# A conditioned block on one core: where the last pair's quarter r3 is summed and gated

## The chip, the cores and the metric

The kernel runs on one core of a Trainium2 chip. The metric is device time in microseconds for one launch; the figure given is the median of several runs. The core's engines are TensorE (PE; its weight loads are shown as PEld), VectorE (DVE), ScalarE (ACT), GpSimd (POOL) and SyncE (SP). SP and ACT issue the transfers.

## The reference

The inputs are `x` of 2 x 2048 x 512 and a condition of 2 x 512, all float32. Cut to what matters:

```python
emb = jnp.dot(jax.nn.silu(t), ada_w) + ada_b
shift_msa, scale_msa, gate_msa, shift_mlp, scale_mlp, gate_mlp = jnp.split(emb, 6, axis=-1)
norm = _ln(x) * (1.0 + scale_msa[:, None]) + shift_msa[:, None]
h = jax.nn.gelu(jnp.dot(norm, ssm_w1) + ssm_b1, approximate=False)
x = x + gate_msa[:, None] * (jnp.dot(h, ssm_w2) + ssm_b2)
norm2 = _ln(x) * (1.0 + scale_mlp[:, None]) + shift_mlp[:, None]
hf = jax.nn.gelu(jnp.dot(norm2, ff_w1) + ff_b1, approximate=True)     # 512 -> 1024
x = x + gate_mlp[:, None] * (jnp.dot(hf, ff_w2) + ff_b2)              # 1024 -> 512
```

The change touches the last line.

## The kernel before, in words

**Tiling.** The 4096 rows of `x` are eight blocks of 512 rows. The first part of the kernel carries each block through the first two products (`ssm1`, `ssm2`). Then the feed-forward part (`ff`) takes the blocks in four pairs, s = 0 to 3: for each pair `up(s)` makes the 1024 hidden columns, and `down(s)` multiplies them by `fw2`. The last pair is s = 3, in the code `last`.

**Fewer products.** Every large product is a 2 x 2 product of quarters done in seven multiplications instead of eight, by Strassen's scheme in Winograd's form, and each of the seven is again done in seven: these inner multiplications are called leaves. In `down` the outer seven run in the order of `DOWN`, P1, P2, P3, P6, P5, P7, P4; the leaves of each run in the order P1, P5, P6, P2, P7, P3, P4. The leaves of two neighbouring outer products alternate on TensorE. A leaf of `down` is two matmuls into a 128 x 256 piece of a PSUM bank. The inner scheme adds some leaves onto others within the bank; six of the seven are read out afterwards. `QUAD` says to which quarter (e, h) of the result each leaf is added. A quarter is complete with the leaf P2, P7, P3 or P4.

**The four sums.** The outer results are collected in `summed`, in SBUF, with the feature on the partitions: r0 is the first half of the output features (d = 0) for the pair's first block, r1 the second half (d = 1) of the first block, r2 d = 1 of the second block, and r3 d = 0 of the second block. Under P1, r1 is set. Under P2, r0 = r1 + P2 is done. Under P3, r3 = P3 is set. Under P6, r1 = r1 + P6. Under P5, r2 = r1 + P5, and when a quarter is complete, r3 = r3 + r2. P7 and P4 end r2 and r1.

**Outputs.** `quarter_out(s, d, blk, r)` sends a finished sum: two passes on ACT apply the gate (scale) and the gated bias (the two values of `columns`), two block transposes on DVE write a band in the tile `far`, four stores write the band to DRAM (`back`), one load brings it back turned (tile `rows`), two additions add the rest of `x` (in `far` or `near`), and the result is stored. In the last pair r0 and r3 go this way, with stores spread over SP and ACT (`queue`). r1 and r2 of the last pair are gated ahead of P7 and P4 by one ACT pass over both, and the leaves of P7 and P4 are then added by `scaled_add`, a multiply-add on DVE that reads the leaf from PSUM. TensorE turns their pieces as they are complete (`turned_by_pe`); DVE adds them to the rest of `x` in the tile `hidden`, and each piece is stored.

**Order.** No order is written by hand. Every instruction is added to `Plan` with the engines that could take it ("vg" is DVE or POOL), a cost in ns, and what it reads and writes. `Plan.order` gives each instruction a latest time, counted back from TensorE's matmuls, whose order is fixed, and from the closing stores, and then simulates the engines: on each engine the instruction with the earliest latest time goes first among those that are ready. A price of `AHEAD` is put on work that DVE could leave to POOL. Additions on DVE and POOL with both inputs in SBUF are kept from running at the same time (`shared`). Each engine then works through its list in that order.

Lines of the profile: L258 is `tt` (additions on DVE or POOL), L276 is `act`, L285 `copy`, L296 `mm`, L306 `turn_by_pe`, L318 `dma`, L1049 `scaled_add`, L1073 the block transposes of `quarter_out`.

Of the kernel before, what the change touches and what calls it, by code (L numbers as in the profile page):

```python
# [11 lines left out]
AF = mybir.ActivationFunctionType  # L12
ALU = mybir.AluOpType
# [187 lines left out]
def kernel(  # L201
# [42 lines left out]
    def cols(ap):  # L244
        n = 1
        for d in ap.shape[1:]:
            n *= d
        return n

    def in_psum(*aps):  # L250
        return any("PSUM" in str(a.space) for a in aps)

    def tt(e, o, a, b, f):
        n, ps = cols(o), in_psum(a, b)
        cost = {"v": n / 0.96 + 70, "g": 2.12 * n + 145}
        plan.add(
            e,
            lambda E: E.tensor_tensor(o, a, b, f),  # L258
            [o],
            [a, b],  # L260
            cost,
            {"v": cost["v"] + 85, "g": cost["g"] + 45},
            "g" if ps else "vg",
        )
# [5 lines left out]
    def act(o, a, func, bias=0.0, scale=1.0):  # L270
        n = cols(o)
        ptrs = [p for p in (bias, scale) if not isinstance(p, float)]
        cost = n / 1.4 + (155, 215, 340)[len(ptrs)]
        plan.add(
            "a",
            lambda E: E.activation(o, a, func, bias=bias, scale=scale),  # L276
            [o],
            [a] + ptrs,
            {"a": cost},
            {"a": cost + 90},  # L280
        )
# [31 lines left out]
    def dma(o, a, q="s", lead=0.0, lat=2000.0, sooner=0.0):  # L313
        size = max(cols(o.unsqueeze(0)), 1) * 4
        outs = [o] if o.tensor.name in scratch else []
        ins = [a] if a.tensor.name in scratch else []
        lead = lead or (0.0 if ins or not outs or size <= plan.LITTLE else 25000.0)
        plan.add(q, lambda E: E.dma_start(out=o, in_=a), outs, ins, {q: plan.ISSUE}, {q: lat}, size=size, lead=lead)  # L318
        plan.ops[-1].sooner = sooner
# [27 lines left out]
    def cut(t, form, **sizes):  # L347
        return t.rearrange(form, **sizes)
# [6 lines left out]
    for n in range(8):  # L355
        t = psum.tile([P, 2 * HT], F32, tag=f"bank{n}", name=f"bank{n}")
# [61 lines left out]
    def thirds(t):  # L418
        return [t[:, n] for n in range(3)]
# [545 lines left out]
    def chain_banks(n):  # L965
        b = {"y": banks[Y_AT[n % 4]], "x": banks[X_AT[n % 2]], "v": banks[V_AT[n % 2]]}
        return b
# [75 lines left out]
    quarters = [0]  # L1043

    def scaled_add(o, t, scale):
        cost = cols(o) / 0.96 + 70
        plan.add(
            "v",
            lambda E: E.scalar_tensor_tensor(o, t, scale, o, ALU.mult, ALU.add),  # L1049
            [o],  # L1050
            [t, o, scale],
            {"v": cost},
            {"v": cost + 85},
        )

    def columns(s, d, e, blk):
        k, b = 2 * d + e, (2 * s + blk) // PER_B
        return gb5[:, k, b : b + 1], mods[5][:, k, b : b + 1]

    def rest_in(s, d, blk, x):  # L1060
        half = slice(d * D // 2, (d + 1) * D // 2)
        dma(x, x1_d[2 * s + blk][:, :, half])
        return x, out_blk[2 * s + blk][:, :, half]

    def quarter_out(s, d, blk, r):
        done = summed[:, r]
        n = quarters[0] % 2
        for e in range(2):
            act(done[:, e], done[:, e], AF.Identity, *columns(s, d, e, blk))
        band = cut(bands[n], "p (a c e r) -> p e c a r", a=M, c=C, e=2)  # L1070
        for e in range(2):
            o, a = band[:, e], cut(done[:, e], "p (c a q) -> p c a q", c=C, a=M)
            plan.add("v", lambda E, o=o, a=a: E.transpose(o, a), [o], [a], {"v": 636}, {"v": 705})  # L1073
        closing = s + 1 == NBLK // 2
        queue = lambda f: "sa"[f % 2] if closing else "s"
        far_t = back_d[s][d][blk]
        for f in range(M):
            dma(far_t[:, f].rearrange("(a q) r -> q a r", a=M), cut(bands[n][f * G : (f + 1) * G], "p (a r) -> p a r", a=M), queue(f))
        flat = done.rearrange("p e t -> p (e t)")
        dma(flat, far_t.rearrange("p f r -> p (f r)"))  # L1080
        x, to = rest_in(s, d, blk, rest[n])
        for h in range(2):
            c = slice(2 * h, 2 * h + 2)
            o = cut(x[:, c], "p c (e f r) -> p (c e) f r", e=2, f=M)
            a = cut(flat, "p (f c e r) -> p c e f r", f=M, c=C, e=2)[:, c].rearrange("p c e f r -> p (c e) f r")
            tt("v" if closing else "vg", o, a, o, ALU.add)
            if closing:
                dma(to[:, c], x[:, c], queue(h))
                plan.closing.append(plan.ops[-1].n)
        if not closing:  # L1090
            dma(to, x)
        quarters[0] += 1

    def down(s):
        q = {f"{o + 1}{blk + 1}": hC[:, blk, :, 2 * o : 2 * o + 2, :] for o in range(2) for blk in range(2)}
        ops = {"P1": q["11"], "P2": q["21"], "P3": q["22"]}
        inner = {}
        last = s + 1 == NBLK // 2

        def sums():  # L1100
            plan.stage = f"ff2 {s}"
            a, b, c = whole_s
            parts("vg", a, q["12"], q["11"], ALU.subtract, 2)
            parts("vg", b, q["22"], a, ALU.subtract, 2)
            parts("vg", q["12"], q["22"], q["12"], ALU.subtract, 2)
            ops.update(P4=c, P5=a, P6=b, P7=q["12"])

        def last_sum():
            plan.stage = f"ff2 {s}"
            parts("vg", ops["P4"], q["21"], ops["P6"], ALU.subtract, 2)  # L1110

        def prepare(n):
            w = ops[DOWN[n]]
            v = {f"{k + 1}{h + 1}": w[:, k, :, h * HT : (h + 1) * HT] for k in range(2) for h in range(2)}
            inner[n] = second(v, thirds(half_s[n % 2]), room=rooms[n % 3] if n < 4 else None)

        def leaf(n, f):
            p = DOWN[n]
            bank = chain_banks(14 * s + 7 + n)
            t = bank[BANK[f]][:, :HT]  # L1120
            for k in range(2):
                mm(t, fw2_leaves[p][f][:, k, :], inner[n][f][:, k, :], f in ("P1", "P5") and k == 0, f in ("P2", "P3", "P4") and k == 1)
            if f == "P1":
                copy(bank["x"][:, :HT], t)
                return
            quad = QUAD[f]
            e, h = int(quad[0]) - 1, int(quad[1]) - 1
            new = f not in ("P7", "P3")
            part = summed[:, :, e, h * HT : (h + 1) * HT]
            r0, r1, r2, r3 = [part[:, r] for r in range(4)]  # L1130

            def add(o, a):
                tt("v", o, t, a, ALU.add)

            if p in ("P1", "P3"):
                o = r1 if p == "P1" else r3
                if new:
                    copy(o, t)
                else:
                    add(o, o)  # L1140
            elif p == "P2":
                add(r0, r1 if new else r0)
                if f == "P4":
                    quarter_out(s, 0, 0, 0)
            elif p == "P6":
                add(r1, r1)
            elif p == "P5":
                add(r2, r1 if new else r2)
                if f in ("P2", "P7", "P3", "P4"):
                    tt("vg", r3, r3, r2, ALU.add)  # L1150
                    if last:
                        act(part[:, 1:3], part[:, 1:3], AF.Identity, *columns(s, 1, e, 0))
                if f == "P4":
                    quarter_out(s, 0, 1, 3)
            elif p == "P7":
                both, wide = part[:, 1:3], t.unsqueeze(1).to_broadcast([P, 2, HT])
                if last:
                    scaled_add(both, wide, columns(s, 1, e, 0)[1])
                else:
                    tt("v", both, wide, both, ALU.add)  # L1160
                if last:
                    turned_by_pe(1, 2, f, quad)
                elif f == "P4":
                    quarter_out(s, 1, 1, 2)
            elif not last:
                add(r1, r1)
                if f == "P4":
                    quarter_out(s, 1, 0, 1)
            else:
                scaled_add(r1, t, columns(s, 1, e, 0)[1])  # L1170
                turned_by_pe(0, 1, f, quad)

        return sums, last_sum, prepare, leaf
# [198 lines left out]
    for i in range(1, NBLK):  # L1372
# [4 lines left out]
        last = i + 2 >= NBLK  # L1377
# [64 lines left out]
```

## Time and profile before

| what | value |
|---|---|
| median of 3 runs | 565.63 us (565.54 to 566.38) |
| the profiled execution | 565.75 us, its span 564.0 us |
| granted TensorE clock, mean | 0.998 |
| PE / DVE / POOL / ACT busy | 98% / 85% / 69% / 50% of the span |
| moved by DMA | 123.68 MB, 219 GB/s in the mean |

The span is the time from the first to the last event of the profiled execution. The busy shares are means over stages with different limits. In rows of the timeline the first number is the start in us from the span's begin, the second the time until the group's end; "x2" merges neighbouring instructions of one kind; the bracket gives the idle time ahead of it and what ended it.

### The profile page before, as it was taken

What the parts mean: (1) busy time and instruction counts of PE and PEld (TensorE: products, weight loads), DVE (VectorE), ACT (ScalarE), POOL (GpSimd) and SP (SyncE); (2) the same over time, 40 slices, a digit from 0 to 9 for tenths busy, and PEclk for the clock granted to TensorE, in tenths of its full rate; (3) what the DMA queues carried; (4) which work ended last, traced back from release to release, by engine and by line L of the source; (5) the groups of instructions that cost most, each with busy time, mean ns of one, the idle gap of its engine ahead of it and who ended that gap; (6) DMA issues with size and microseconds to landing.
All of it is one profiled execution on the core that took longest, in us unless ns stands there. A gap on an engine that the chain in (4) does not pass through costs nothing.

```text
span 564.0 us, 8729 instructions
## 1 busy us (share of the span) xinstructions
PE 552.8 (98%) x2809; PEld 481.2 (85%) x2809; DVE 481.4 (85%) x842; ACT 281.7 (50%) x521; POOL 388.5 (69%) x475
## 2 busy tenths in 40 slices
PE   8999999999999999999999999999999999999994
PEld 4888889888898988888878888888888888888883
DVE  5696978888778588899999997799988999988896
ACT  3474867674877855556206347315338314335230
POOL 2887747979935399984746777676768677767650
PEclk9999999999999999999999999999999999999999
DMA  8953799988399969994202899602998503984317
GB/s 314 399 223 84 239 347 308 331 257 269 103 289 327 302 272 265 329 284 159 74 2 53 295 328 336 190 4 69 317 318 308 183 9 103 319 267 144 95 36 224
DMA packets 66033, 123.68 MB, mean 219 GB/s; under 512 B 5652, under 2 KB 33220, under 8 KB 64452
## 3 DMA queue, kind: packets, MB, share of 16 engines
q1 hardware_dynamic: 63696, 121.53, 65.5%
q10 hardware_dynamic: 2292, 1.60, 1.0%
q8 instruction: 22, 0.36, 0.2%
q14 instruction: 23, 0.19, 0.1%
HBM read 77.89 MB, written 44.18 MB: 216 GB/s over the span
## 4 chain that ended last, share of the span: by engine, by line
PE 87%; DVE 7%; DMA 3%; ACT 1%; issue 1%; POOL 1%; DVEq 0%; SPq 0%; ACTq 0%
PE bank L296 87%; DVE rows L258 2%; DMA fw<-in_L_cond_ada_w_dram 1%; DVE near L258 1%; DVE rows L1049 1%; DVE fw L258 1%; DMA rows<-back 1%; DVE far L258 1%; DVE far L1073 1%; ACT rows L276 1%; DVE hidden L258 0%; DMA fw<-in_L_cond_ada_b_dram 0%; PE bank L306 0%; POOL hidden L258 0%; POOL near L258 0%
## 5 line engine op out<-in xcount | busy, mean ns | idle before, releaser
L296 PE MATMUL bank<-turned,ring 128*128 128x256 f32 x896 | 210.2, 380 | 0.2 <-DVE turned L660 0.2
L296 PEld LDWEIGHTS bank<-turned,ring 128*128 128x128 f32 x896 | 167.9, 190 | 23.2 <-DVE turned L660 0.4
L258 DVE TENSOR_TENSOR hidden<-bank,hidden 128x512 f32<-128x512 f32 (+2 forms) x178 | 126.2, 738 | 23.8 <-PE bank L296 20.3
L296 PE MATMUL bank<-near,hidden 128*128 128x256 f32 (+1 forms) x470 | 95.1, 350 | 0.0
L296 PEld LDWEIGHTS bank<-near,hidden 128*128 128x128 f32 x470 | 82.2, 190 | 9.4 <-POOL near L258 0.3
L258 POOL TENSOR_TENSOR turned<-turned 128x512 f32<-128x512 f32 (+1 forms) x65 | 73.6, 1145 | 22.3 <-DVE turned L258 10.2
L296 PE MATMUL bank<-far,fw 128*128 128x256 f32 (+1 forms) x354 | 86.0, 374 | 0.2
L296 PE MATMUL bank<-ring 128*128 128x256 f32 x336 | 82.7, 380 | 0.1
L258 DVE TENSOR_TENSOR rows<-bank,rows 128x256 f32<-128x256 f32 (+1 forms) x142 | 66.0, 478 | 15.5 <-PE bank L296 12.6
L296 PEld LDWEIGHTS bank<-far,fw 128*128 128x128 f32 x354 | 66.5, 190 | 9.6 <-POOL fw L258 0.5
L285 ACT COPY bank<-bank 128x512 f32<-128x512 f32 (+2 forms) x84 | 37.7, 449 | 73.6 <-PE bank L296 67.1
L296 PEld LDWEIGHTS bank<-ring 128*128 128x128 f32 x336 | 63.5, 190 | 9.9 <-ACT bank L285 0.5
L258 POOL TENSOR_TENSOR hidden<-hidden 128x128 f32<-128x128 f32 (+2 forms) x46 | 46.9, 1029 | 28.4 <-DVE hidden L258 13.3
L276 ACT ACTIVATE hidden<-hidden,cols 128x512 f32<-128x512 f32 (+1 forms) x66 | 44.4, 709 | 42.2 <-DVE hidden L258 42.1
L296 PE MATMUL bank<-near,fw 128*128 128x256 f32 (+1 forms) x246 | 60.6, 376 | 0.0
L296 PE MATMUL bank<-hidden,fw 128*128 128x256 f32 (+1 forms) x216 | 53.3, 376 | 0.2
L296 PEld LDWEIGHTS bank<-near,fw 128*128 128x128 f32 x246 | 46.3, 190 | 6.1
L276 ACT ACTIVATE turned<-turned,mod,mod 128x512 f32<-128x512 f32 x56 | 42.4, 807 | 8.7 <-DMA turned<-turned 8.3
L296 PEld LDWEIGHTS bank<-hidden,fw 128*128 128x128 f32 x216 | 40.2, 190 | 6.3 <-issue 0.9
L258 POOL TENSOR_TENSOR fw<-fw 128x256 f32<-128x256 f32 (+1 forms) x38 | 35.6, 945 | 11.5 <-DMA fw_parts<-fw 4.0
L258 POOL TENSOR_TENSOR ring<-turned,ring 128x256 f32<-128x256 f32 x41 | 29.8, 739 | 16.8 <-PE bank L296 14.6
L276 ACT ACTIVATE rows<-rows,gb,mod 128x512 f32<-128x512 f32 x32 | 25.7, 812 | 27.0 <-DVE rows L258 18.8
(123 smaller groups left out, 734.3 us busy)
## 6 DMA issues: line engine op xcount, KB each, us to landing
ring<-fw_parts SPq DMA_DIRECT2D x28, 512.0 KB, 4.1
turned<-far SPq DMA_DIRECT2D x52, 256.0 KB, 4.0
ring<-fw_parts SPq DMA_DIRECT2D x28, 384.0 KB, 5.4
turned<-turned SPq DMA_DIRECT2D x32, 256.0 KB, 5.1
rows<-back SPq DMA_DIRECT2D x14, 512.0 KB, 5.9
back<-far SPq DMA_DIRECT2D x52, 128.0 KB, 3.0
fw_parts<-fw SPq DMA_DIRECT2D x21, 256.0 KB, 4.9
fw<-in_L_cond_ada_w_dram SPq DMA_DIRECT2D x5, 1024.0 KB
```

The costliest lines, as they stand in the source:

```text
L258: lambda E: E.tensor_tensor(o, a, b, f),
L276: lambda E: E.activation(o, a, func, bias=bias, scale=scale),
L285: plan.add("a", lambda E: E.copy(o, a), [o], [a], {"a": cost}, {"a": cost + 60})
L296: lambda E: E.matmul(o, lhsT, rhs, start=start, stop=stop, skip_group_check=True, **kw),
L1049: lambda E: E.scalar_tensor_tensor(o, t, scale, o, ALU.mult, ALU.add),
L1073: plan.add("v", lambda E, o=o, a=a: E.transpose(o, a), [o], [a], {"v": 636}, {"v": 705})
```

## The change

In the last pair, when a quarter of r1 = P1 + P6 is complete (under P6), r3 += r1 is done at once, on DVE or POOL, and an ACT pass applies gate and bias to that quarter of r3. Under P5 each leaf is then read twice from PSUM: by a multiply-add onto r3 (`scaled_add` with the gate of d = 0 and the second block), and by the addition into r2 as before. The addition r3 += r2 and the two ACT passes in `quarter_out` for r3 fall away in the last pair. The other pairs keep their instructions. Two costs of the planner are changed: a tanh Gelu pass by +30 ns, a `scaled_add` by +50 ns (in all pairs). The order of all engines is planned anew from this.

```diff
@@ act
-        cost = n / 1.4 + (155, 215, 340)[len(ptrs)]
+        cost = n / 1.4 + (155, 215, 340)[len(ptrs)] + (30 if func == AF.Gelu_apprx_tanh else 0)
@@ scaled_add
-        cost = cols(o) / 0.96 + 70
+        cost = cols(o) / 0.96 + 120
@@ quarter_out
-    def quarter_out(s, d, blk, r):
+    def quarter_out(s, d, blk, r, scaled=False):
         done = summed[:, r]
         n = quarters[0] % 2
-        for e in range(2):
+        for e in range(0 if scaled else 2):
             act(done[:, e], done[:, e], AF.Identity, *columns(s, d, e, blk))
@@ leaf of down
-            new = f not in ("P7", "P3")
+            new, full = f not in ("P7", "P3"), f in ("P2", "P7", "P3", "P4")
...
             elif p == "P6":
                 add(r1, r1)
+                if last and full:
+                    tt("vg", r3, r3, r1, ALU.add)
+                    act(r3, r3, AF.Identity, *columns(s, 0, e, 1))
             elif p == "P5":
+                if last:
+                    scaled_add(r3, t, columns(s, 0, e, 1)[1])
                 add(r2, r1 if new else r2)
-                if f in ("P2", "P7", "P3", "P4"):
+                if full and last:
+                    act(part[:, 1:3], part[:, 1:3], AF.Identity, *columns(s, 1, e, 0))
+                elif full:
                     tt("vg", r3, r3, r2, ALU.add)
-                    if last:
-                        act(part[:, 1:3], part[:, 1:3], AF.Identity, *columns(s, 1, e, 0))
                 if f == "P4":
-                    quarter_out(s, 0, 1, 3)
+                    quarter_out(s, 0, 1, 3, last)
```

## The prediction

> **What bounds the kernel now.** I read the page's busy line first, then busy time by stretch, then the chain that ended last, then VectorE's (DVE's) timeline of the last 35 us.
>
> ```profile
> span 564.0 us, 8729 instructions
> PE 552.8 (98%) x2809; PEld 481.2 (85%) x2809; DVE 481.4 (85%) x842; ACT 281.7 (50%) x521; POOL 388.5 (69%) x475
> ```
>
> ```profile
> 480.00:530.00 50.00, 49.98 (x232) 43.69 (x231) 45.27 (x62) 20.51 (x38) 34.32 (x31) 1.00 0.66 220
> 530.00:535.40 5.40, 5.40 (x26) 4.75 (x26) 4.39 (x7) 0.73 (x2) 3.73 (x2) 1.00 0.41 100
> 535.40:540.60 5.20, 5.20 (x25) 4.56 (x24) 4.97 (x9) 0.36 (x1) 3.70 (x3) 1.00 0.29 101
> 540.60:545.90 5.30, 5.30 (x25) 4.37 (x23) 5.16 (x9) 2.88 (x4) 3.09 (x4) 1.00 0.00 0
> 545.90:550.90 5.00, 4.86 (x25) 4.06 (x24) 4.90 (x10) 1.99 (x4) 1.67 (x2) 1.00 0.01 3
> 550.90:557.00 6.10, 5.13 (x29) 4.19 (x28) 5.90 (x16) 0.00 (x0) 0.00 (x0) 1.00 0.89 204
> 557.00:564.00 7.00, 0.17 (x2) 0.00 (x0) 2.04 (x4) 0.00 (x0) 0.00 (x0) 0.80 0.82 270
> ```
>
> The columns are length, then busy time of PE, PEld, DVE, ACT, POOL, clock, DMA share, GB/s. Up to 545.9 TensorE has no gap, so nothing earlier can be won by order alone. From 535.4 to 557 DVE is busy for 20.93 of 21.6 us: the tail belongs to DVE.
>
> ```profile
> 519.83 22.68 PE bank L296 x105
> 553.69 0.41 DVE rows L1049
> 554.35 4.38 DMA rows<-back
> 558.83 0.69 DVE near L258
> 559.52 0.60 DVEq L1437
> ```
>
> In this chain TensorE hands over to DVE at 542.5, DVE to the load of a turned quarter (`rows<-back`), and that to the two last additions (`near`), which are the quarter r3: d=0 of the pair's second block, the one that `quarter_out(s, 0, 1, 3)` sends. Its output ends the kernel. The steps, and what lies between them:
>
> ```profile
> 533.03 0.42 DVE L258 TENSOR_TENSOR rows<-bank,rows 128x256 f32<-128x256 f32 x1 [0.77 <-PE bank L296]
> 539.65 1.29 DVE L258 TENSOR_TENSOR rows<-rows 128x256 f32<-128x256 f32 x1
> 540.87 1.21 DVE L258 TENSOR_TENSOR near<-hidden,near 128x1024 f32<-128x1024 f32 x1
> 542.99 0.82 DVE L258 TENSOR_TENSOR rows<-rows 128x256 f32<-128x256 f32 x1
> 543.48 0.91 POOL L258 TENSOR_TENSOR rows<-rows 128x256 f32<-128x256 f32 x1
> 543.73 1.22 DVE L258 TENSOR_TENSOR far<-near,far 128x512 f32<-128x512 f32 x1
> 544.87 0.41 DVE L258 TENSOR_TENSOR rows<-bank,rows 128x256 f32<-128x256 f32 x1
> 545.20 0.73 DVE L1049 SCALAR_TENSOR_TENSOR rows<-bank,mod,rows 128x512 f32<-128x512 f32 x1
> 545.86 0.72 DVE L258 TENSOR_TENSOR rows<-rows 128x256 f32<-128x256 f32 x1
> 546.05 0.73 PEld L296 LDWEIGHTS bank<-hidden,fw 128*128 128x128 f32 x4 [0.51 <-issue]
> 546.50 2.25 DVE L1049 SCALAR_TENSOR_TENSOR rows<-bank,mod,rows 128x512 f32<-128x512 f32 x3
> 546.61 0.81 ACT L276 ACTIVATE rows<-rows,gb,mod 128x512 f32<-128x512 f32 x1 [0.55 <-DVE rows L258]
> 547.63 0.81 ACT L276 ACTIVATE rows<-rows,gb,mod 128x512 f32<-128x512 f32 x1
> 548.67 1.29 DVE L1073 STREAM_TRANSPOSE far<-rows 128x512 f32<-128x512 f32 x2
> 549.99 0.78 SPq L318 DMA_DIRECT2D back<-far  x2
> 550.00 0.85 ACTq L318 DMA_DIRECT2D back<-far  x2
> 550.85 0.47 DVE L1049 SCALAR_TENSOR_TENSOR rows<-bank,mod,rows 128x256 f32<-128x256 f32 x1
> 551.24 0.41 DVE L258 TENSOR_TENSOR hidden<-bank,hidden 128x256 f32<-128x256 f32 x1
> 553.72 0.40 SPq L318 DMA_DIRECT2D out_dram<-far  x1
> 554.60 0.48 DVE L1049 SCALAR_TENSOR_TENSOR rows<-bank,mod,rows 128x256 f32<-128x256 f32 x1
> 556.99 0.76 DVE L258 TENSOR_TENSOR hidden<-bank,hidden 128x256 f32<-128x256 f32 x2 [0.20 <-PE bank L306]
> 558.83 1.29 DVE L258 TENSOR_TENSOR near<-rows,near 128x512 f32<-128x512 f32 x2 [1.08 <-DMA rows<-back]
> 560.15 0.38 ACTq L318 DMA_DIRECT2D out_dram<-near  x1
> ```
>
> The last leaf of the fifth product is added to r2 at 544.87. r3 += r2 follows at 545.86, ACT's gate at 546.61 and 547.63, the two transposes at 548.67 (after three multiply-adds of the next product), four stores to `back` at 549.99, the load at 554.35, two additions at 558.83 to 560.12, and the last store is issued at 560.15. From there to the end of the span are 3.85 us. The other output, the quarter turned by TensorE, has its last addition over at 557.75 (556.99 + 0.76). So r3 is 2.37 us later than its neighbour on DVE.
>
> The profiled execution took 565.75 us with this span, so 1.75 us lie around it. The median of the runs is 565.63, 0.12 below. I work in differences of the span and take them from the median.
>
> **The change part by part.**
>
> *Removed from the fifth product (P5):* four additions r3 += r2. Three ran on DVE; from each start to the next DVE start they took 540.87 - 539.65 = 1.22, 543.73 - 542.99 = 0.74 and 546.50 - 545.86 = 0.64, together 2.60 us. One ran on POOL (0.91). Also the two 128x512 gate passes of r3 on ACT, 0.81 each, which go from the path.
>
> *Added in the fifth product:* six multiply-adds of 128x256 that read the leaf from PSUM a second time. The same form starts at 550.85 and its successor at 551.24, so each takes 0.39 us of DVE: 6 x 0.39 = 2.34 us. The PSUM bank is now free only after both readers. Behind each stand the next evictions in DVE's queue, and TensorE's later leaves wait for those; three of the six take the place of the removed additions (3 x 0.39 = 1.17 against 2.60), so from 539.65 on DVE gets no more to do, rather less.
>
> *Added in the product before it (P6, the fourth in order):* four additions r3 += r1 (128x256, on DVE or POOL), in about 533 to 540, at the prices above: 0.64 to 1.22 on DVE, 0.91 on POOL. With the old split, three on DVE, they cost 2.60 there. And four gate passes of 128x256 on ACT, each under the 0.81 of the 128x512 form; ACT is busy 0.73 + 0.36 us between 530 and 540.6, so they are hidden by its idling and cost nothing. If that cover went, up to 0.81 us of ACT would stand ahead of a multiply-add, and behind that one in DVE's queue the evictions that TensorE's next leaves need.
>
> *DVE's balance:* +2.34 - 2.60 + 2.60 = +2.34 us with the old split. Against that stand DVE's gaps in 530 to 540.6, 1.01 + 0.23 = 1.24 us, and POOL's, 1.67 + 1.50 = 3.17 us, enough for three of the additions (2.73). Lower end: all four additions on POOL, 2.34 - 2.60 = -0.26 us, and when the other three multiply-adds too vanish in the gaps, 1.17 - 2.60 = -1.43. Upper end: nothing absorbed, +2.34. POOL is mostly busy with additions that DVE could also do and that hold the two up (the same shape took 1.29 and 0.72 us on DVE), so I take neither end: the gaps absorb 1.24 and one more addition goes to POOL (-0.87, a third of 2.60). That leaves +0.23.
>
> A page speaks against this step. The Trainium skill, "VectorE: DVE Perf Modes", section "Rules for kernel authors", says not to fuse chained vector operations for speed, and to keep the number of operations low. Here the six evictions and four additions become sixteen instructions instead of ten, and by the rule the sum would take the whole +2.34; that case is a rival below.
>
> *Moved: r3's path.* The addition and ACT's gate leave it. With the last multiply-add where the last addition stood (544.87), r3 would be ready at about 545.3 and the transposes 3.4 us earlier (548.67 - 545.3). That is the best end. The worst is zero, when other DVE work goes first, as the three multiply-adds at 546.50 do now. I take 2.05: the multiply-add at 545.20 and one of the three are wanted by TensorE just as early (its weight load at 546.05 stood 0.51 us behind the first), and each takes 545.86 - 545.20 = 0.66, so the transposes start at 545.3 + 1.32 = 546.62. Every DMA of the path moves along: four stores on SP and ACT, one load on SP, two output stores; their number and sizes stay. On SP the load must pass the stores of outputs that now stand ahead of it, the one for `far` at 553.72 the last. If the order lets it, the load lands at 558.73 - 2.05 = 556.68, in the midst of the other quarter's last additions.
>
> *The end:* r3's two additions then no longer wait 1.08 us behind an idle DVE, but they still have to be done, and DVE has no room for them before 557 (5.90 of 6.10 us busy). DVE ends at 557.75 + 1.29 - 0.20 (the gap at 556.99, filled) + 0.23 = 559.07 instead of 560.12: 1.05 us less. With the last store right behind it and 3.85 us after that, as now, the span is 562.95. The stores run in a rush there:
>
> ```profile
> 557.00:558.00 1.00, 0.17 (x2) 0.00 (x0) 0.75 (x2) 0.00 (x0) 0.00 (x0) 1.00 0.93 340
> ```
>
> The load's 512 KB moves out of it, worth 0.52 MB / 340 GB/s = 1.5 us at most; but two stores of 256 KB then share the time with those of the other quarter, so I leave the 3.85 as it is.
>
> *The planner's costs:* 50 ns more for a multiply-add and 30 ns more for the tanh form of Gelu change no instruction, only the order.
>
> ```profile
> L276 ACT ACTIVATE hidden<-hidden,cols 128x512 f32<-128x512 f32 x48 | 32.6, 715 | 33.7 <-DVE hidden L258 33.6
> ```
>
> ACT idled 33.7 us in front of these 48 passes, so it does not matter when they are planned to end by some tens of ns. TensorE has no gap to win there (49.98 of 50 us), and for a loss the nearest row is the 0.51 us at 546.05. I take zero from between zero and +0.5.
>
> *Sum:* -1.05 us on the span, 565.63 - 1.05 = 564.58, so 564.6. A measurement of this kernel tells about 0.2% (1.13 us) from no change: the forecast lies right at that bound.
>
> **The rivals.**
>
> *A clear gain.* The additions under P6 and the first three multiply-adds vanish in the gaps of 530 to 540.6, and DVE's lower end holds: 1.43 us less work after 539.65, enough for r3's 1.29. Then TensorE's last transposes set the end (DVE waited for them at 556.99), at 557.75 as now if the load lands by 555.4 (the best end of 3.4 us), later if it lands at 556.68. I take the middle between 557.75 and the forecast's 559.07, 558.4. The span is 558.4 + 3.85 = 562.25, a gain of 1.7: 563.9; at 557.75 it would be 563.2. For it: POOL's 3.17 us. Against it: 4.97 of 5.20 us on DVE in the second half of that stretch.
>
> *Held by the queue on SP: nothing gained.* The load at 554.35 followed a store that DVE's addition had released, issued at 553.72 and over at 554.12. If the load keeps its place behind this store, an earlier transpose is worth nothing, and the time is 565.6. For it: the chain names DVE and SP ahead of the load, not the stores to `back`. Against it: the order is planned anew, and the load's inputs are there earlier.
>
> *Slower: DVE stands in line behind the band.* DVE works in order. If the two additions of r3 are queued ahead of the other quarter's multiply-add at 554.60, because the planner thinks the load lands by then, DVE stands until 556.68 with 557.75 - 554.60 = 3.15 us of work behind. It would end at 556.68 + 1.29 + 3.15 + 0.23 = 561.35 instead of 560.12, so 566.9. It decides from where the load lands later than about 556.6 with the additions queued at that place; each us later costs one more. For it: today's load takes 4.38 us, in the rush of stores. Against it: the additions of the first quarter (the store at 553.72 sends them) were queued long after their data came, so the planner gives such work little urgency.
>
> *Slower by count:* nothing is absorbed, +2.34 in place of +0.23. DVE ends at 558.84 + 2.34 = 561.18, a loss of 1.06: 566.7. For it: the 20.93 of 21.6 us. Against it: the gaps and POOL's idle time. The Trainium skill's rule on the number of operations asks for this one.
>
> **How the numbers follow.** The forecast's case has 0.50, halved by the bound: 0.25 faster, 0.25 the same. The clear gain has 0.18. The queue on SP has 0.14, all the same. DVE in line has 0.10, all slower. The count has 0.08, half of it the same and half slower. Together: faster 0.43, the same 0.43, slower 0.14. The range reaches from 563.4, which leaves out only the last of the clear gain (563.2, some 0.03), to 566.3, which takes in the queue's case and those of the count in which a fifth or more is absorbed, and leaves out DVE in line: 0.10 + 0.04. That is 0.17 outside. The forecast's own range is 564.0 to 565.2.
>
> **What would show it.** Right: no ACT pass between the last multiply-add of the fifth product and r3's transposes; the transposes near 546.6; six multiply-adds of 128x256 more, with 0.39 us from start to start; the load issued ahead of the first quarter's store on SP; no idle DVE in front of the `near` additions; the last store issued near 559.1. Wrong: the load still at 554; DVE idle for over a microsecond with `rows<-back` as what ended it, and evictions behind; gaps on TensorE before 545; or a chain that ends in the quarter turned by TensorE, with the same last store's time.

## The result and the profile after

The changed kernel takes 564.89 us (564.49 to 565.21, 20 runs) against 565.84 us (565.46 to 566.38, 20 runs) before: 0.95 us less, a ratio of 0.9984 with a 95% interval of 0.9978 to 0.999. Run once more beside the last experiments it took 564.93 us, ratio 0.9982 (0.9973 to 0.9991). The profiled execution took 564.89 us with a span of 563.1. The medians are over all executions; in four sets of runs one execution went at a lower granted clock (0.66 in the one of 836.55 us of the changed kernel), and the ratios leave these out.

Busy time by stretch in the changed kernel (length, then PE, PEld, DVE, ACT, POOL, clock, DMA share, GB/s), the two stretches in which the tail is made:

```profile
535.40:545.90 10.50, 10.50 (x51) 9.14 (x50) 9.17 (x20) 4.91 (x8) 9.75 (x7) 1.00 0.14 51
545.90:557.00 11.10, 9.91 (x53) 8.08 (x51) 10.16 (x23) 1.17 (x2) 3.73 (x4) 1.00 0.57 139
```

Over the same stretches DVE had 20.93 us before and has 9.17 + 10.16 = 19.33 now, though it runs six multiply-adds more. POOL had 3.70 + 3.09 + 1.67 = 8.46 and has 13.48: two additions of 128x1024 into `near` that DVE did there are now POOL's. But the work is mostly moved in time, not taken away. DVE is busier ahead of the tail, 5.37 us against 4.39 in 530 to 535.4 and 45.92 against 45.27 in 480 to 530, so that from 480 to 557 it has 70.62 us now and 70.59 before; and POOL runs 475 instructions in both kernels.

The chain that ended last, in order of time, from where it leaves TensorE:

```profile
519.89 27.00 PE bank L296 x125
546.89 0.02 issue
...
548.72 3.63 DMA back<-far
552.36 0.67 DVE far L258
553.02 0.41 DVE rows L1049
...
553.64 4.22 DMA rows<-back
557.85 0.02 issue
557.88 0.69 DVE near L258
```

TensorE now carries the chain to 546.89 (542.51 before): the stop at 546.05 is gone. From there the page runs over r3's transposes and stores to `back`, and then, as before, over the additions of the first quarter (`far`) into the load `rows<-back`. The step from the stores to those additions is no wait: the first addition started 0.40 us behind the multiply-add ahead of it on DVE (551.94 and 552.34), the same step as in the next such pair (552.94 and 553.33, 0.39), and it reads nothing of r3. A second trace of the same kernel leads into the same addition from TensorE:

```profile
518.89 28.70 PE bank L296 x133
...
550.89 0.88 PE bank L296 x4
...
552.20 0.68 DVE far L258
552.88 0.41 DVE rows L1049
```

So TensorE's pace sets when the first quarter is done. Its weight loads stood still for DVE twice in the kernel before, for 0.51 us at 546.05 and once more (the first row here), and once in the changed kernel (the second row):

```profile
550.98 0.21 PEld L306 LDWEIGHTS bank<-far,rows 128*128 128x128 f32 x2 [0.30 <-DVE hidden L258]
548.65 0.20 PEld L306 LDWEIGHTS bank<-far,rows 128*128 128x128 f32 x2 [0.23 <-DVE rows L258]
```

What lies behind comes 0.66 to 0.67 us earlier: the first quarter's addition 552.34 against 553.01, the last additions of the quarter turned by TensorE 556.33 against 556.99. The timeline of DVE, SP and ACT:

```profile
542.94 3.00 DVE L1049 SCALAR_TENSOR_TENSOR rows<-bank,mod,rows 128x256 f32<-128x256 f32 x5
545.86 0.70 DVE L1073 STREAM_TRANSPOSE far<-rows 128x512 f32<-128x512 f32 x1
547.59 0.70 DVE L1073 STREAM_TRANSPOSE far<-rows 128x512 f32<-128x512 f32 x1
548.32 0.78 SPq L318 DMA_DIRECT2D back<-far  x2
552.34 0.68 DVE L258 TENSOR_TENSOR far<-rows,far 128x512 f32<-128x512 f32 x1
553.05 0.40 SPq L318 DMA_DIRECT2D out_dram<-far  x1
553.64 0.34 SPq L318 DMA_DIRECT2D rows<-back  x1
556.33 0.76 DVE L258 TENSOR_TENSOR hidden<-bank,hidden 128x256 f32<-128x256 f32 x2 [0.20 <-PE bank L306]
557.88 1.29 DVE L258 TENSOR_TENSOR near<-rows,near 128x512 f32<-128x512 f32 x2 [0.79 <-DMA rows<-back]
559.20 0.38 ACTq L318 DMA_DIRECT2D out_dram<-near  x1
```

The stores to `back` are issued at 548.32, 1.67 us earlier than before. The load is issued only 0.71 us earlier (553.64 against 554.35), right behind the first quarter's store on SP, which itself moved from 553.72 to 553.05. It takes 4.22 us (4.38 before). The last store is issued at 559.20, 0.95 us earlier, and from there it is 3.9 us to the end, as before. So r3's transfer lost 0.96 of its 1.67 us in SP's queue, and DVE still idles 0.79 us in front of the last two additions.

### The profile page after: what moved, and what is told of

Its sections match the earlier page's. It is cut to its first block, busy times and chain, and to the rows that moved or that the text cites. A ratio compares the mean times of both kernels' runs of the same rounds, so it can differ in the third digit from the quotient of the medians.

```text
span 563.1 us, 8745 instructions
## 1 busy us (share of the span) xinstructions
PE 552.2 (98%) x2809; PEld 481.2 (85%) x2809; DVE 479.8 (85%) x848; ACT 282.6 (50%) x523; POOL 384.7 (68%) x475
## 4 chain that ended last, share of the span: by engine, by line
PE 89%; DVE 6%; DMA 3%; issue 0%; POOL 0%; DVEq 0%; SPq 0%; ACTq 0%; POOLq 0%
PE bank L296 88%; DVE rows L258 2%; DMA fw<-in_L_cond_ada_w_dram 1%; DVE near L258 1%; DVE far L258 1%; DMA rows<-back 1%; DVE fw L258 1%; DMA back<-far 1%; PE bank L306 0%; DMA fw<-in_L_cond_ada_b_dram 0%; DVE far L1073 0%; DVE hidden L258 0%; POOL far L258 0%; POOL fw L258 0%; POOL rows L258 0%
## 5 line engine op out<-in xcount | busy, mean ns | idle before, releaser
L258 POOL TENSOR_TENSOR turned<-turned 128x512 f32<-128x512 f32 (+1 forms) x62 | 70.4, 1146 | 20.6 <-DVE turned L258 9.1
L258 POOL TENSOR_TENSOR hidden<-hidden 128x128 f32<-128x128 f32 (+2 forms) x45 | 43.5, 976 | 25.8 <-DVE hidden L258 13.0
L276 ACT ACTIVATE rows<-rows,gb,mod 128x512 f32<-128x512 f32 (+1 forms) x34 | 26.7, 787 | 36.9 <-DVE rows L258 25.0
```

## The experiments

Two readings were open. One is the forecast's: r3's path became shorter, and what DVE has left to do sets the end. The other: the load of r3 stands in SP's queue behind the first quarter's store, and the end moves with that store, whatever r3's path does. And the costs of the planner might have done all of it. The ratio is always to the kernel before on the same chip, where that took 565.74 to 565.84; it need not be the quotient of the two medians. The last three columns are from each profiled execution. Two of these took longer than their kernel's median, by 0.4 us (gate late, load on ACT: 564.73) and 0.8 (load on ACT, six reads more: 567.33), and their columns are late by about as much. "Costs alone" and "old costs" are explained below.

| kernel | median us | ratio (95%) | load issued | last store issued | span |
|---|---|---|---|---|---|
| before | 565.84 | | 554.35 | 560.15 | 564.0 |
| changed | 564.89 | 0.9984 (0.9978 to 0.999) | 553.64 | 559.20 | 563.1 |
| costs alone | 565.48 | 0.9993 (0.998 to 1.0005) | 554.07 | 559.96 | 563.8 |
| old costs | 565.58 | 0.9993 (0.9983 to 1.0003) | 554.54 | 559.96 | 563.7 |
| old Gelu cost | 566.63 | 1.0013 (1.0004 to 1.0022) | 555.34 | 561.25 | 565.1 |
| changed, load on ACT | 564.35 | 0.997 (0.9958 to 0.9983) | 552.31 | 558.28 | 562.5 |
| before, load on ACT | 566.22 | 1.0003 (0.9994 to 1.0013) | 555.36 | 561.36 | 564.6 |
| before, r0's stores on ACT | 565.59 | 0.9996 (0.9988 to 1.0005) | 554.16 | 559.84 | 563.7 |
| gate late | 565.13 | 0.9987 (0.9978 to 0.9996) | 553.63 | 559.37 | 563.3 |
| gate late, load on ACT | 564.32 | 0.9972 (0.9962 to 0.9983) | 552.71 | 558.73 | 562.9 |
| load on ACT, six reads more | 566.5 | 1.0011 (1.0002 to 1.002) | 555.55 | 561.59 | 565.5 |
| gate late, six reads more | 565.6 | 0.9992 (0.9983 to 1.0001) | 554.17 | 559.76 | 563.7 |

**The load on ACT's queue, in the changed kernel.**

```diff
-        dma(flat, far_t.rearrange("p f r -> p (f r)"))
+        dma(flat, far_t.rearrange("p f r -> p (f r)"), "a" if closing and r == 3 else "s")
```

> The changed kernel with one edit: the last pair's load of the turned quarter r3 is issued by ACT, not SP. The order on DVE is the same as in the changed kernel. Theory of the queue on SP: the stores to back had landed by 552.4, the load (553.64) stood behind the first quarter's store (553.05 to 553.45). Then it is issued near 552.4, lands near 556.7, DVE does not idle in front of the last two additions, which start at 557.1 instead of 557.88: 0.8 us gained, 564.1. Theory of DVE's work or of the rush of transfers: nothing is gained, 564.9, because the load takes longer or the stores behind it do.

It took 564.37 us, ratio 0.9967 (0.9957 to 0.9978). A second set of runs gave the trace:

> The changed kernel with r3's load on ACT's queue once more, for its trace; the first time 564.4, 0.5 us under the changed kernel. Theory of the queue on SP: the load is issued near 552.4 instead of 553.64, and DVE does not idle in front of the near additions; the last store is issued 0.8 us earlier than 559.20. That only 0.5 us came of it would then lie behind the last issue: 3.9 us to the end in the changed kernel, here some 4.2, as the stores of both quarters meet. Theory of the rush alone: the load is issued earlier but takes as much longer.

```profile
552.31 0.35 ACTq L318 DMA_DIRECT2D rows<-back  x1
556.29 0.76 DVE L258 TENSOR_TENSOR hidden<-bank,hidden 128x256 f32<-128x256 f32 x2 [0.20 <-PE bank L306]
556.96 1.28 DVE L258 TENSOR_TENSOR near<-rows,near 128x512 f32<-128x512 f32 x2
558.28 0.38 ACTq L318 DMA_DIRECT2D out_dram<-near  x1
```

The load is issued 1.33 us earlier with DVE's order unchanged, the additions follow without a gap, and the last store goes 0.92 us earlier. Shown: SP's queue held the load. With it free, DVE comes to the last two additions straight from the other quarter's (556.29), which now set the end. Of the 0.92 us, 0.54 came out in the time (564.35 against 564.89; the intervals of the two ratios just overlap, but 564.37 and, with the gate late, 564.32 were measured too). The rest went behind the last issue, 562.5 - 558.28 = 4.2 us instead of 3.9. The transfers then ran at (stretches of this kernel)

```profile
556.00:558.00 2.00, 0.47 (x4) 0.23 (x3) 1.80 (x5) 0.00 (x0) 0.00 (x0) 1.00 1.10 349
558.00:560.00 2.00, 0.00 (x0) 0.00 (x0) 0.24 (x1) 0.00 (x0) 0.00 (x0) 1.00 1.07 329
```

as the second expectation had it: the stores of both quarters share the time. That this makes the end longer is likely, not shown; the changed kernel's transfers run at 345 to 359 GB/s in 557 to 560.

**The same edit in the kernel before.**

> The kernel before with the same edit: the load of r3 on ACT's queue. The stores to back are issued 1.67 us later here (549.99 against 548.32) and land 3.3 to 4 us after, near 553.7 to 554.0, so the load can start at most 0.3 to 0.6 us before its 554.35. Theory of the queue on SP: 0.2 to 0.5 us gained, about 565.4, less than with the same edit in the changed kernel; the difference of the two edits is what the earlier r3 is worth when nothing holds the load. Theory of DVE's work: no change, 565.8.

A miss in the other direction: the load was issued later, at 555.36. The median is 566.22 beside 565.83 for the kernel before on that chip, which the interval (0.9994 to 1.0013) does not tell from nothing; the loss shows in the trace.

```profile
554.76 0.40 ACTq L318 DMA_DIRECT2D out_dram<-far  x1
555.36 0.42 ACTq L318 DMA_DIRECT2D rows<-back  x1
560.03 1.29 DVE L258 TENSOR_TENSOR near<-rows,near 128x512 f32<-128x512 f32 x2 [2.23 <-DMA rows<-back]
```

The expectation left out ACT's list. There the planner put the load behind the second store of the first quarter, which waits for the later of its two additions. It is the same hold in another queue: 1.01 us later at the issue, 1.21 at the last store, 0.6 in the span.

**The first quarter's stores both on ACT, in the kernel before.**

```diff
-                dma(to[:, c], x[:, c], queue(h))
+                dma(to[:, c], x[:, c], "a" if r == 0 else queue(h))
```

> The kernel before with both output stores of the first quarter (tile far) on ACT's queue, so that r3's load on SP stands behind no store of that quarter; the order on DVE is unchanged. Theory of the queue on SP: the load waits only for the stores to back, issued until 550.85; it moves from 554.35 to 553.7 to 554.1, and the time by 0.1 to 0.4 us, to about 565.6. If the held load had been the whole reason for the time before, it would move by 1 us or more, to 564.8. If nothing but DVE counts, 565.8.

```profile
550.39 3.64 DMA back<-far
554.04 0.02 SPq L318
...
554.16 4.27 DMA rows<-back
```

Now the chain names the stores to `back` ahead of the load. It gains 0.19 us at the issue, and the median is 565.59 beside 565.74 on that chip, which the interval does not tell from nothing. In the kernel before, then, the stores and the queue released the load almost together; in the changed kernel the queue is 1.33 us too late. The earlier r3 is what made the hold worth removing.

**The two costs alone, and the change without them.** The first sets the costs of the change (`act` +30 for the tanh Gelu, `scaled_add` 70 to 120) in the kernel before; the second takes both back from the changed kernel.

> The kernel before with the two planner costs of the change alone (a tanh Gelu pass +30 ns, a multiply-add +50 ns). DVE's order changes only in the last pair. If the gain of the change (0.95 us) lies in the moved sum and gate, this stays at the time before, 565.8 within 0.3 us. If it lies in the order that the new costs bring (TensorE's stop of 0.51 us at 546.05 gone, evictions earlier), this reaches 565.3 or better, and then the stop at 546 must be gone in its trace.

> The changed kernel with the two old planner costs. If the gain lies in the moved sum and gate, this is at 564.9 like the changed kernel. If it lies in the order from the new costs, 565.8 or worse; the multiply-adds are then planned 50 ns too short, twelve more of 128x256 and six of 128x512, so DVE can be 0.3 to 0.9 us later than planned at 550.

565.48 and 565.58, beside 565.83: each lies between its two expectations, neither is told from no change, and the two gains of the medians, 0.35 and 0.25, make 0.60, not 0.95. The traces say more. With the costs alone the stop of TensorE is still there (the first row below), though the transposes come 0.7 us earlier (547.99) and the load 0.28. Without the costs a worse stop appears on TensorE's weight loads (the second row):

```profile
546.15 0.73 PEld L296 LDWEIGHTS bank<-hidden,fw 128*128 128x128 f32 x4 [0.50 <-DVE rows L1049]
541.28 0.73 PEld L296 LDWEIGHTS bank<-near,fw 128*128 128x128 f32 x4 [1.79 <-DVE rows L1049]
```

and the timeline of DVE in that kernel says why:

```profile
540.75 0.48 DVE L1049 SCALAR_TENSOR_TENSOR rows<-bank,mod,rows 128x256 f32<-128x256 f32 x1 [0.34 <-ACT rows L276]
```

The multiply-add waits for ACT's early gate, which waits for the addition r3 += r1, and TensorE waits for the bank that the multiply-add reads. The changed kernel has such a wait too, 0.33 us at 539.10, but only one, and no stop of TensorE; here there are two, and three of the four additions run on DVE instead of two. r3's transposes are over at 549.96 us before, 549.28 with the costs alone, 549.94 with the change alone, and 548.29 with both. Only with both is there no such stop, and only then do the transposes come by the whole 1.67 us earlier.

**The old Gelu cost only.**

```diff
-        cost = n / 1.4 + (155, 215, 340)[len(ptrs)] + (30 if func == AF.Gelu_apprx_tanh else 0)
+        cost = n / 1.4 + (155, 215, 340)[len(ptrs)]
```

> The changed kernel with the Gelu cost of before and the new cost of the multiply-add. With both old costs 565.6 was measured, with a stop of TensorE of 1.79 us at 541 that DVE's wait for the gate passes made; with both new ones 564.9. DVE's order follows the old Gelu cost from about 500 us on and differs from the kernel with both old costs only in the last rows. If the Gelu cost brings the good order, the stop is still there and the time is 565.4 to 565.8; if the multiply-add's cost does, 564.9 and no stop. My forecast had the costs at nothing.

```profile
541.40 0.73 PEld L296 LDWEIGHTS bank<-near,fw 128*128 128x128 f32 x4 [1.80 <-DVE rows L1049]
554.05 0.68 DVE L258 TENSOR_TENSOR far<-rows,far 128x512 f32<-128x512 f32 x1
555.34 0.34 SPq L318 DMA_DIRECT2D rows<-back  x1
```

566.63: 1.7 us over the changed kernel, slower than the kernel before, and worse than either expectation. So the order without the stop needs the Gelu cost; whether that cost is enough without the multiply-add's was not run. It reaches back into the last pair's first half: in 480 to 530 us POOL has 27.84 us of work with it in the changed kernel, 34.32 in the kernel before. The multiply-add's cost without it is worse than neither: r0's additions on DVE come 0.80 us later than with both old costs (554.05 against 553.25), the load with them (555.34 against 554.54), and the time follows, 1.05 us more, though TensorE's stop is the same.

**The addition moved, the gate left late.** r3 += r1 stays ahead of the fifth product, its leaves are added plainly, and `quarter_out` gates r3 with two ACT passes as before.

```diff
                 if last and full:
                     tt("vg", r3, r3, r1, ALU.add)
-                    act(r3, r3, AF.Identity, *columns(s, 0, e, 1))
...
-                    scaled_add(r3, t, columns(s, 0, e, 1)[1])
+                    add(r3, r3)
...
-                    quarter_out(s, 0, 1, 3, last)
+                    quarter_out(s, 0, 1, 3)
```

> The changed kernel with the addition r3 += r1 still moved ahead, but the gate left where it was: the leaves of the fifth product are added plainly, and two ACT passes of 0.8 us stand between them and r3's transposes. Theory of the queue on SP: r3's stores to back come about 1.2 us later than 548.32 and land near 553.6, just about when the first quarter's store frees SP (553.45), so little is lost: 565.0 to 565.2. My forecast's theory, in which each us of r3's path is worth as much: 1.2 us lost, 566.0.

```profile
545.00 0.81 ACT L276 ACTIVATE rows<-rows,gb,mod 128x512 f32<-128x512 f32 x1 [0.46 <-DVE rows L258]
545.82 0.70 DVE L1073 STREAM_TRANSPOSE far<-rows 128x512 f32<-128x512 f32 x1
546.88 0.75 DVE L1049 SCALAR_TENSOR_TENSOR rows<-bank,mod,rows 128x512 f32<-128x512 f32 x1 [0.36 <-PE bank L296]
547.55 0.70 DVE L1073 STREAM_TRANSPOSE far<-rows 128x512 f32<-128x512 f32 x1
```

565.13 us, as the theory of the queue had it, but not for its reason: both expectations had the transposes later, and they are not. The gate passes end by 545.81, while DVE is still at leaves, and DVE's order puts other multiply-adds between the transposes anyway. The medians with the early and the late gate lie 0.24 us apart, within the intervals. In the traces the load is issued at the same time, 553.63 against 553.64, and 0.17 us of difference at the last store come from the load itself, 4.39 us against 4.22. With the load on ACT added, so that nothing holds it:

> The gate left late, and r3's load on ACT's queue. The transposes of r3 start at the same times with the gate early or late (545.86 and 547.59; 545.82 and 547.55). Theory that the order of DVE, not r3's readiness, sets the transposes: this equals the changed kernel with the load on ACT, 564.3 to 564.6. Theory that the early gate and the multiply-adds pay once the load is free: 564.9 or more.

564.32 us, the same as with the early gate (564.35).

**Six reads more on DVE.** Each leaf of the fifth product is read from PSUM once more, into a tile that nobody reads (`add(spoil, r3)` behind the leaf's other reads), first in the changed kernel with the load on ACT:

> The changed kernel with r3's load on ACT's queue and, under the fifth product, six additions more on DVE: each leaf is read a third time from PSUM, into a tile nobody reads. To be held against the same kernel without them (564.4). They cost 0.33 to 0.41 us each, 2.0 to 2.5 us in all. Rule of the count: all of it shows, 566.4 to 566.9. Theory of the gaps: DVE idled 0.33, 0.76, 0.36 and 0.24 us between 538.8 and 552 and POOL takes over additions; 0.2 to 0.9 us show, 564.6 to 565.3.

566.5 us, 2.15 more, as by the count. But its trace, of an execution of 567.33 us, shows another reason beside the count: DVE waits for the early gate, and TensorE for DVE. (The execution had also lost time ahead of the tail, where TensorE waited 0.61 us for a load at 498.28; the changed kernel's trace has no such wait.)

```profile
541.59 0.48 DVE L1050 SCALAR_TENSOR_TENSOR rows<-bank,mod,rows 128x256 f32<-128x256 f32 x1 [1.25 <-ACT rows L276]
542.68 1.10 PE L296 MATMUL bank<-near,fw 128*128 128x256 f32 x4 [1.86 <-DVE quads L258]
```

So it settles nothing on the count. The same six reads where no gate pass stands in front of a leaf:

> The kernel of the experiment with the gate left late, with six additions more on DVE under the fifth product (each leaf is read once more from PSUM, into a tile nobody reads), so that no multiply-add waits for a gate pass of ACT. To be held against the kernel without them, 565.13. They are worth 0.33 to 0.41 us each, 2.0 to 2.5 us. Rule of the count: all of it shows, 567.1 to 567.6. Theory of the gaps: DVE there idles 0.81, 0.19, 0.36 and 0.26 us between 541 and 552, 1.6 us in all, and some work can go to POOL; 0 to 0.9 us show, 565.1 to 566.0.

565.6 us, 0.47 more than without them, for six reads of 0.33 to 0.41 us. The two were held against the kernel before on different chips, and by the ratios (0.9992 and 0.9987) it is 0.3; either is far from 2.0. Between 530 and 557 us DVE is busy only 0.71 us longer (25.58 against 24.87 with the gate late), though TensorE's matmuls stop for 0.29 us at 540.20. Part of the reads fell into DVE's gaps, POOL took over an addition of 128x512, and one of 128x256 got shorter (its price is at the end of this document). The theory of the gaps holds here. For the 2.15 us of the other kernel the wait for the gate, with TensorE's stop of 1.86 us behind it, is the likely reason; the two kernels also differ in the load's queue, so its share is not measured.

The changed kernel itself, beside these:

> The changed kernel itself, to hold these beside it on the same chip: 564.9, 0.95 us under the kernel before.

It took 564.93 us.

## Why the prediction was right

The forecast was 564.6, and 0.95 us were gained where 1.05 were forecast. The number holds better than its way there.

- *The tail belongs to DVE, nothing is won earlier:* TensorE runs 0.06 us later up to the tail (519.89 against 519.83), so the whole gain lies behind. Right as to the place. As to the engine only half: without the stop TensorE carries the chain far into the tail, to 546.89 in one trace and to 551.77 in the other.
- *DVE's balance, +0.23 us:* mis-sized. POOL took one more of the four additions, as forecast, but also other sums: from 530 to 557 DVE has 24.70 us instead of 25.32, that is -0.62, and 1.6 less in 535.4 to 557.
- *The planner's costs, nothing:* this term was wrong. With the old Gelu cost the same instructions take 566.63 us. DVE has about as little to do in 535.4 to 557 there, 9.22 + 10.20 = 19.42 us, as in the changed kernel (19.33), so the amount of DVE's work does not decide the time; the order does, and whether TensorE stops in it.
- *r3's path, 2.05 us:* the transposes end at 548.29, forecast 546.62 + 1.29 = 547.91. But the shorter path is not why. With the gate late they start at the same times, so the removed gate passes were covered by DVE's other work. What is left is the addition taken out of the fifth product, together with the order.
- *The load, if the order lets it:* this step failed. Forecast was the issue at 554.35 - 2.05 = 552.30; it was 553.64. The rival of the queue on SP described the mechanism, but its price, no gain, was wrong: the store in front moved forward by 0.67 us itself, as r0's additions on DVE did. With the queue free the load went at 552.31.
- *The end:* forecast was DVE at work without a gap until 559.07; it idles 0.79 us for the load and ends at 557.88 + 1.29 = 559.17. A load 1.34 us later than forecast and less work on DVE than forecast met in nearly the same end. That is luck in the sum, not in the place.
- *Slower by count:* did not happen. The Trainium skill's rule in "VectorE: DVE Perf Modes" ("Rules for kernel authors") to keep the number of operations low does not price this tail: the change runs six instructions more on DVE and is faster, and six reads more, 2.0 to 2.5 us by the count, cost 0.47 us where DVE had gaps.
- *DVE in line behind the band:* did not happen; the planner put the `near` additions behind everything else on DVE.

In eight of the twelve kernels in the table DVE idles 0.77 to 2.23 us for the load ahead of the last two additions. In these the span ends 9.2 to 9.8 us after the load's issue, while that issue ranges from 553.63 to 555.36: there the load's issue is a better measure of the tail than any engine's work. In the other four (old costs, and the three with both the load on ACT and the changed order) DVE comes to these additions 0.67 us after the other quarter's last additions start, without a gap, and the end follows TensorE and DVE.

What stays open: the gain's share between the moved addition and the costs. The costs alone gave 0.35 us and the change without them 0.25, each within its interval, and together they give 0.95; each of the kernels is planned anew as a whole, and one with the old addition and the new order of the rest was not tried.

## What to carry to other kernels

Where a chain of transfers ends the kernel, look at what stands ahead of each transfer in its own queue, and on every queue that it could go to: a shorter path in front of a held transfer shows only as far as the holder moves. Before paying engine work to take a step out of a path, look whether the step was covered; here the gate's passes were, and the early gate even stopped TensorE in orders in which its input came late. With a planner, a cost of a few tens of ns is an edit of its own: run it alone, and run the change without it.

## What the runs showed of the hardware

Behind the last issue the end is not a fixed time: 3.2 us in the kernel before with the load on ACT (564.6 - 561.36), 3.9 us in both kernels, and 4.2 us in two of the three kernels with the changed order and the load on ACT. In the third of these, with six reads more, it is 3.9 us. What it depends on is not shown. So moving the load alone came out at the end by a half to two thirds: 0.92 us at the last issue gave 0.6 in the span, and 1.21 us lost cost 0.6; the change itself got its 0.95 us in full. An addition of two SBUF tiles of 128x256 took 0.42 us on DVE while POOL idled, and 1.43 us while POOL had a 2.36 us addition running; it ended 0.29 us after POOL's. Another in the changed kernel took 1.35 us (from 534.30) and ended 0.28 us after a POOL addition (534.10 to 535.37). (The first row is from the kernel with the gate late and six reads more, the others from the changed kernel.)

```profile
535.92 0.42 DVE L258 TENSOR_TENSOR rows<-rows 128x256 f32<-128x256 f32 x1
537.01 1.43 DVE L258 TENSOR_TENSOR rows<-rows 128x256 f32<-128x256 f32 x1
535.79 2.36 POOL L258 TENSOR_TENSOR near<-hidden,near 128x1024 f32<-128x1024 f32 x1 [0.43 <-PE bank L296]
```
